# Queries of a latent attention for two batches in one matmul, and its transposed weights in half tiles

## The chip, the cores and the metric

The kernel runs on one core of a Trainium2 chip, as one program. A time is the device time of one execution in microseconds (us). A profile is one execution recorded by the hardware profiler; its span runs from the first to the last instruction.

## What is computed

Two transformer layers on 8 batches of 100 tokens with 512 features: cross attention, a mixture of experts, a second cross attention and a quantised feed-forward layer. The change lies in the second attention ("attention 2"). Cut to it, with b the batch, s the token, l one of 361 context rows, h one of 16 heads, r one of 64 features:

```python
q_r    = einsum('bshq,hqr->bhsr', q_big, W_qr)       # queries, 64 a head
k_r    = einsum('bld,hdr->bhlr', kv_rope, W_kr)      # keys of the turned context
scores = einsum('bhsr,bhlr->bhsl', q_r, k_r)
attn   = softmax(scores)                             # over the 361 rows
ctx_c  = einsum('bhsl,bld->bhsd', attn, kv_rope)
out    = einsum('bhsd,hkd->bshk', ctx_c, w_kc_kv).reshape(b, s, H * K) @ Wo.T
x      = x + out
```

The kernel does not form k_r. It multiplies each head's query by W_kr, which gives a query of 128 features that is scored against the context row itself. That multiplication is what the code calls `queries`.

## The kernel before, in words

Everything is float32 here. `qr` holds the 64 features of all 16 heads for all 800 tokens: even heads in partitions 0 to 63, odd heads in partitions 64 to 127, eight pairs of heads along the second axis. It lies in the upper half of `ctxT`, the tile in which the attention's result is built; a batch's result overwrites the batch's own query columns. `wkr_sb` holds W_kr in the same arrangement.

Attention 2 goes through the batches one after the other (the loop `for b in range(B)`). For a batch:

- `queries(b)` (line 1294): for each of two halves, four pairs of heads; for each pair two matmuls, one with the upper and one with the lower 64 partitions (line 1300; 128 weight columns, 100 moving columns), into two PSUM banks, one for each parity. VectorE copies the even bank (line 1304), ScalarE the odd one (line 1305) into `qe`, 1600 columns: first eight even heads, then eight odd ones. So a batch has 16 matmuls, of which each is two passes of TensorE and two records of the trace, and four copies of 128x400.
- The 1600 columns are cut into 13 tiles, 12 of 128 columns and one of 64 (`BTILES`). `scores` (line 1310): one matmul of the tile's queries against the context columns `kvT`, 361 wide (line 1312); VectorE takes the negative row maximum (line 1314); ScalarE the exponential with its row sum (line 1318); VectorE the reciprocal (line 1320); then VectorE for odd tiles, GpSimd for even ones, multiplies (line 1321).
- `weights_transposed` (line 1324): three transpositions on TensorE (line 1327) and one copy into `pT`, a tile of 3 x 1600 columns, of which there are two.
- `values` (line 1330): when four heads' 400 columns of `pT` are there, three matmuls (line 1333) with the context rows, and a copy into `ctxT`. A batch has four such groups, j = 0 to 3.

The copies of `weights_transposed` and `values` go through `evacuate` (line 77): VectorE (line 80) and ScalarE (line 82) take turns by a counter that runs on over the batches. A batch has 13 + 4 such copies.

The loop runs three tiles ahead: after the scores of tile i, `drain(3)` does the transpositions of tile i - 3, and values that became ready are done with the next transposition. `queries(b + 1)` stands after tile 8 of batch b (after tile 2 in batch 0), and the next context columns are turned after tile 10. In batches 1 and on, after tiles 3 and 9, a late weight block of the feed-forward layer is quantised on VectorE (lines 133 to 145), nine blocks in all.

In this stretch the order written by hand is not enforced: the tile framework's scheduler orders the instructions of each engine when the program is built (the sections before it and the end of the kernel are under `tc.manual_schedule`). Engines run their lists in order and wait for each other on semaphores. [...] After the loop the values are projected (lines 357 and 363) and the feed-forward layer follows.

Of the kernel before, what the change touches and what calls it, by code (L numbers as in the profile page):

```python
# [12 lines left out]
F32 = mybir.dt.float32  # L13
# [6 lines left out]
P = 128  # L20
B, S, D = 8, 100, 512
# [18 lines left out]
NH1, R1, CQ = 16, 64, 384  # L40
LC, LP = 3, 121
# [9 lines left out]
def tile_kernel(  # L51
# [7 lines left out]
    nc = tc.nc  # L59

    def open_pool(name, bufs=1, side="left"):
        guard = tc.tile_pool(name=name, bufs=bufs, side=side)
        pool = guard.__enter__()
        return pool, lambda: guard.__exit__(None, None, None)
# [6 lines left out]
    def bank(dtype=F32):  # L71
        cols = 512 if dtype == F32 else 1024
        return psum.tile([P, cols], dtype, tag="bank", name="bank")
# [3 lines left out]
    def evacuate(dst, src):  # L77
        turn[0] += 1
        if turn[0] % 2:
            nc.vector.tensor_copy(dst, src)  # L80
        else:
            nc.scalar.copy(dst, src)  # L82
# [342 lines left out]
    def columns_of_weights(b):  # L425
        return weights_columns(soft.pop(b)[1])
# [27 lines left out]
    pT = columns_of_weights(0)  # L454
# [3 lines left out]
    for b in range(2, 6):  # L458
# [3 lines left out]
        pT = columns_of_weights(b - 1)  # L462
# [239 lines left out]
    def fold_head(i, wq_p, kq_p, qr_p, j, pa=None):  # L702
        pa = bank() if pa is None else pa
        for c in range(CQ // P):
            nc.tensor.matmul(  # L705
                pa[:, ts(j, R1)], kq_p[:, j, c, :], qr_p[:, j, c, :],
                start=(c == 0), stop=(c == CQ // P - 1),
            )
        return pa

    def fold_copy(i, wq_p, kq_p, qr_p, pa):
        a_p = fw.tile([P, 2 * R1], F32, tag="a_p", name=f"a_p{i}", bufs=2)
        nc.scalar.copy(a_p, pa[:, : 2 * R1])
        return i, wq_p, a_p

    def fold_first(*loads):
        pa = fold_head(*loads, 0)
        return fold_copy(*loads, fold_head(*loads, 1, pa))

    def fold_second(i, wq_p, a_p):  # L720
        pb = bank()
        for j in range(2):
            nc.tensor.matmul(  # L723
                pb[ds(R1 * j, R1), :], a_p[:, ts(j, R1)], wq_p[:, j, :], start=True, stop=True
            )
        f_p = fw.tile([P, D], F32, tag="f_p", name=f"f_p{i}", bufs=2)
        nc.scalar.copy(f_p, pb)
        return i, f_p
# [14 lines left out]
    pT = columns_of_weights(5)  # L743
# [9 lines left out]
    pT = columns_of_weights(6)  # L753
# [12 lines left out]
    pT = columns_of_weights(7)  # L766
# [13 lines left out]
    part = fold_first(*loaded.pop(0))  # L780
# [6 lines left out]
    part = fold_second(*part)  # L787
# [29 lines left out]
    wkr_sb = qw.tile([P, NH1 // 2, DC], F32, tag="wkr", name="wkr_sb")  # L817
# [68 lines left out]
    with tc.If(spills > 0, preferred_fallthrough_block=False):  # L886
# [12 lines left out]
        for e in range(NE):  # L899
# [3 lines left out]
            for t, r in enumerate(ROWS):  # L903
                pt = bank().rearrange("p (c q) -> p c q", c=KC)
# [7 lines left out]
                for m, (m0, mr) in enumerate(HCH):  # L912
                    pw = bank()
                    ups = [(0, UP[m], mr)] if m < 2 else [(0, UP64, 64), (64, HE, 32)]
                    for j, cols in enumerate(([(0, m0, mr)], ups)):
                        a = sp.tile([P, KC, P], F32, tag=f"sp{j}", name=f"sp{j}_{e}_{t}_{m}")
# [5 lines left out]
                        for c in range(KC):  # L922
                            nc.tensor.matmul(
                                pw[:mr, ds(j * P, r)], a[:, c, :mr], xT[:, c, :r],
                                start=(c == 0), stop=(c == KC - 1),
# [111 lines left out]
    part = fold_copy(*loads, fold_head(*loads, 1, pa))  # L1037
    following = fold_first(*loaded.pop(0))
    part = fold_second(*part)
# [6 lines left out]
    for e in range(NE):  # L1046
# [35 lines left out]
        part = None  # L1082
        gate_and_up(0)
        if loaded:
            part = fold_first(*loaded.pop(0))
# [4 lines left out]
        if part:  # L1090
            part = fold_second(*part)
# [90 lines left out]
    qr = ctxT[:, NH1 // 2 :, :]  # L1182
# [21 lines left out]
    for b in range(B):  # L1204
        kv = contexts.pop(0)
        kvr = rot.tile([LP, LC, DC], F32, tag="turned", name=f"turned{b}", bufs=2)
# [11 lines left out]
    def context_rows(b):  # L1218
        kvr = kvp.tile([LP, LC, DC], F32, tag="kvr", name=f"kvr{b}")
        d = nc.sync.dma_start(kvr, ctx_rot[b])  # L1220
        context_load[0] = d.ins
        return kvr

    def context_columns(b, kvr):
        pt = bank()[:, : LC * LP].rearrange("p (c l) -> p c l", c=LC)
        for c in range(LC):
            nc.tensor.transpose(pt[:, c, :], kvr[:, c, :], ident[:LP, :LP])
        kvT = kvp.tile([P, L], F32, tag="kvT", name=f"kvT{b}")
        nc.scalar.copy(kvT[:, :LP], pt[:, 0, :])
        nc.vector.tensor_copy(  # L1230
            kvT[:, LP:].rearrange("p (c l) -> p c l", c=LC - 1), pt[:, 1:, 1:]
        )
        return kvT
# [22 lines left out]
    for g, tiles in enumerate(GROUPS):  # L1256
# [3 lines left out]
        more = g + 1 < len(GROUPS)  # L1260
        if more:
            token_norms(GROUPS[g + 1])
        for p0 in range(0, NH1 // 2, per):
            pq = bank()[:, : per * n].rearrange("p (i q) -> p i q", i=per)
            for i in range(per):
                for c in range(KC):
                    nc.tensor.matmul(  # L1267
                        pq[:, i, :], wqf[:, c, ts(p0 + i, P)], xT[:, c, :],
                        start=(c == 0), stop=(c == KC - 1),
# [9 lines left out]
    kvr = context_rows(0)  # L1279
    kvT = context_columns(0, kvr)  # L1280
# [3 lines left out]
    a1w, close_a1w = open_pool("attn1w", bufs=2)  # L1284
# [4 lines left out]
    HP = NH1 // 2  # L1289
    BROWS = NH1 * S  # L1290
    BTILES = [(k, min(P, BROWS - k)) for k in range(0, BROWS, P)]
    VC = 4 * S

    def queries(b):
        qe = a1w.tile([P, 2, HP * S], F32, tag="qe", name=f"qe{b}")
        for half in range(2):
            pe = [bank(), bank()]
            for i in range(4):
                for par in range(2):
                    nc.tensor.matmul(  # L1300
                        pe[par][:, ts(i, S)], wkr_sb[ds(R1 * par, R1), 4 * half + i, :],
                        qr[ds(R1 * par, R1), 4 * half + i, ts(b, S)], start=True, stop=True,
                    )
            nc.vector.tensor_copy(qe[:, 0, ts(half, VC)], pe[0][:, :VC])
            nc.scalar.copy(qe[:, 1, ts(half, VC)], pe[1][:, :VC])
        return qe.rearrange("p a q -> p (a q)")

    of_scores = []

    def scores(qe, kvT, k0, r, odd):  # L1310
        ps = bank()
        nc.tensor.matmul(ps[:r, :L], qe[:, ds(k0, r)], kvT, start=True, stop=True)  # L1312
        nm = small.tile([P, 1], F32, tag="nm", name="nm")
        d = nc.vector.tensor_reduce(nm[:r], ps[:r, :L], AX.X, ALU.max, negate=True)  # L1314
        of_scores.append(d.ins)
        e = a1w.tile([P, L], F32, tag="e", name="e", bufs=4)
        sm = small.tile([P, 1], F32, tag="sm1", name="sm1")
        nc.scalar.activation(e[:r], ps[:r, :L], AF.Exp, bias=nm[:r], accum_out=sm[:r])  # L1318
        rs = small.tile([P, 1], F32, tag="rs1", name="rs1")
        nc.vector.reciprocal(rs[:r], sm[:r])  # L1320
        (nc.vector if odd else nc.gpsimd).tensor_scalar_mul(e[:r], e[:r], rs[:r])  # L1321
        return e

    def weights_transposed(e, pT, k0, r):
        pt = bank()[:, : LC * P].rearrange("p (c q) -> p c q", c=LC)
        for c in range(LC):
            nc.tensor.transpose(pt[:LP, c, :r], e[:r, ds(c * (LP - 1), LP)], ident[:r, :r])  # L1327
        evacuate(pT[:, :, ds(k0, r)], pt[:LP, :, :r])

    def values(b, j, kvr, pT):  # L1330
        pc = bank()
        for c in range(LC):
            nc.tensor.matmul(  # L1333
                pc[:, :VC], kvr[:, c, :], pT[:, c, ts(j, VC)], start=(c == 0), stop=(c == LC - 1)
            )
        evacuate(
            ctxT.rearrange("p (i a) q -> p i a q", a=2)[:, ts(j % 2, 4), j // 2, ts(b, S)],
            pc[:, :VC].rearrange("p (i q) -> p i q", i=4),
        )
# [5 lines left out]
    def drain(n):  # L1345
        while len(late) > n:
            late.pop(0)()

    def behind(b, i, e, kvr, pT):
        k0, r = BTILES[i]  # L1350
        weights_transposed(e, pT, k0, r)
        while ready:
            values(*ready.pop(0))
        for j in range(NH1 // 4):
            if k0 < (j + 1) * VC <= k0 + r:
                ready.append((b, j, kvr, pT))

    qe = queries(0)
    for b in range(B):
        more = b + 1 < B  # L1360
        pT = a1w.tile([LP, LC, BROWS], F32, tag="pT", name=f"pT{b}")
        if more:
            kvr_next = context_rows(b + 1)
        for i, (k0, r) in enumerate(BTILES):
            e = scores(qe, kvT, k0, r, i % 2)
            late.append(lambda a=(b, i, e, kvr, pT): behind(*a))
            drain(3)
            if more and i == (8 if b else 2):
                qe_next = queries(b + 1)

            if b and i in (3, 9) and late_loads:
                n, w = late_loads.pop(0)
                with tc.issue_after(of_scores[8]):
                    turn_gate_up(*quantise_gate_up(n, w, a1w))
                if n + 2 < OT:
                    with tc.issue_after(context_load[0]):
                        late_loads.append(load_gate_up(n + 2, a1w))
            if more and i == 10:
                kvT_next = context_columns(b + 1, kvr_next)
        if more:  # L1380
            qe, kvr, kvT = qe_next, kvr_next, kvT_next
    drain(0)
    values(*ready.pop(0))
    close_a1w()
# [11 lines left out]
    pt = bank()  # L1396
# [213 lines left out]
    for k, t in enumerate(order):  # L1610
# [8 lines left out]
        if k >= 2:  # L1619
            q, sh = hidden_q.pop(order[k - 2])  # L1620
# [17 lines left out]
    q, sh = hidden_q.pop(last)()  # L1638
# [8 lines left out]
    q, sh = hidden(t, sx, xqT, True)  # L1647
# [81 lines left out]
```

## Time and profile before

| what | value |
|---|---|
| median of 3 runs | 683.59 us (680.39 to 683.71) |
| the profiled execution | 684.2 us |
| its span | 682.5 us |
| granted TensorE clock, mean | 0.981 |
| attention 2, from the first query matmul to the last values | 345.6 to about 539.8 us |
| a batch, from one query block to the next (479.14 to 503.11) | 24.0 us |

How to read the profile. Engines are PE (TensorE matmul), PEld (its weight load), DVE (VectorE), ACT (ScalarE), POOL (GpSimd) and SP (the queue that issues most DMAs). The page gives the busy time of each with its share and the number of instructions, and the chain that ended last: followed back from the last instruction, at each step to what released it. A row of a group of instructions has line, engine, operation, what it writes and reads, shape and count, then busy time in us, mean duration of one in ns, and idle time ahead of it with the releaser. Matmuls are pipelined, so the mean duration of one (272 ns for a query matmul record) is far more than the step from one start to the next; the busy time of the group divided by its count is nearer to what it costs. A wait row reads: who, for whom, total us, how often, longest. A row of the chain reads: start, us, what. A row of the windows reads: window, its length, busy time and count of each engine, granted clock, DMA share, GB/s.

### The profile page before, as it was taken

What the parts mean: (1) busy time and instruction counts of PE and PEld (TensorE: products, weight loads), DVE (VectorE), ACT (ScalarE), POOL (GpSimd) and SP (SyncE); (2) the same over time, 40 slices, a digit from 0 to 9 for tenths busy, and PEclk for the clock granted to TensorE, in tenths of its full rate; (3) what the DMA queues carried; (4) which work ended last, traced back from release to release, by engine and by line L of the source; (5) the groups of instructions that cost most, each with busy time, mean ns of one, the idle gap of its engine ahead of it and who ended that gap; (6) DMA issues with size and microseconds to landing.
All of it is one profiled execution on the core that took longest, in us unless ns stands there. A gap on an engine that the chain in (4) does not pass through costs nothing.

```text
span 682.5 us, 10210 instructions
## 1 busy us (share of the span) xinstructions
PE 647.0 (95%) x3637; PEld 417.3 (61%) x3637; DVE 420.7 (62%) x1059; ACT 245.2 (36%) x557; POOL 184.1 (27%) x197
## 2 busy tenths in 40 slices
PE   8999997499998999999999999999999999999995
PEld 6767755367765677568866666666666644444442
DVE  4875698326665453254168877776676356566687
ACT  3654444141221211231155555455555322221140
POOL 2222231601110022138424243324333102221021
PEclk9999999589999999999999999999999999999998
DMA  8700293699999999664200211110000120111211
GB/s 303 237 17 18 99 331 108 244 301 190 271 288 321 322 254 275 131 193 122 63 1 17 57 44 42 31 35 12 1 11 1 46 83 8 30 29 30 49 37 61
DMA packets 80312, 80.41 MB, mean 118 GB/s; under 512 B 41283, under 2 KB 54135, under 8 KB 80127
## 3 DMA queue, kind: packets, MB, share of 16 engines
q1 hardware_dynamic: 76543, 70.97, 35.8%
q0 software_dynamic: 3712, 8.72, 6.6%
q8 instruction: 30, 0.49, 0.3%
q14 instruction: 27, 0.22, 0.1%
HBM read 56.36 MB, written 16.50 MB: 107 GB/s over the span
## 4 chain that ended last, share of the span: by engine, by line
PE 65%; DVE 7%; DMA 3%; POOL 2%; issue 2%; ACT 1%; SPq 0%; POOLq 0%; ACTq 0%; DVEq 0%
PE bank L357 12%; PE bank L1053 10%; PE bank L1333 10%; PE bank L1312 7%; PE bank L1267 6%; PE bank L1117 5%; PE bank L1327 4%; PE bank L1457 3%; POOL e L1321 2%; PE bank L1300 2%; DVE nm L1314 1%; PE bank L705 1%; PE bank L723 1%; DMA dn<-in_wdn 1%; PE bank L985 1%
## 5 line engine op out<-in xcount | busy, mean ns | idle before, releaser
L1321 POOL TENSOR_SCALAR e<-e,rs 128x361 f32<-128x361 f32 (+1 forms) x56 | 67.3, 1203 | 134.9 <-DVE rs L1320 134.2
L357 PE MATMUL bank<-wvo,ctxT 128*128 128x512 f32 x192 | 83.9, 593 | 0.0
L1312 PE MATMUL bank<-kvT,qe 128*128 128x361 f32 (+1 forms) x208 | 82.0, 477 | 0.0
L1053 PE MATMUL bank<-xgT,w 128*128 128x240 f32 (+1 forms) x384 | 76.5, 371 | 1.6 <-ACT xgT L989 0.9
L1053 PEld LDWEIGHTS bank<-xgT,w 128*128 128x128 f32 (+1 forms) x384 | 63.8, 181 | 16.7 <-issue 9.0
L1333 PE MATMUL bank<-pT,kvr 121*128 121x400 f32 x192 | 70.4, 502 | 1.8 <-DVE pT L80 1.8
L1318 ACT ACTIVATE e<-bank,nm 128x361 f32<-128x361 f32 (+1 forms) x104 | 58.7, 564 | 29.8 <-DVE nm L1314 21.0
L1327 PEld LDWEIGHTS bank<-ident,e 128*121 128x121 f32 (+1 forms) x312 | 47.3, 183 | 33.7 <-POOL e L1321 7.8
L1314 DVE TENSOR_REDUCE nm<-bank 128x1 f32<-128x361 f32 (+1 forms) x104 | 54.9, 528 | 20.3 <-PE bank L1312 19.2
L357 PEld LDWEIGHTS bank<-wvo,ctxT 128*128 128x128 f32 x192 | 36.2, 190 | 43.1 <-issue 42.6
L1128 POOL DMA_INDIRECT x_acc<-y,place x16 | 24.4, 1525 | 128.5 <-ACT y L1127 125.0
L1327 PE MATMUL bank<-ident,e 128*121 128x128 f32 (+1 forms) x312 | 52.8, 279 | 2.1 <-POOL e L1321 2.1
L1474 POOL TENSOR_TENSOR hid<-g,u 128x512 f32<-128x512 f32 (+1 forms) x17 | 20.5, 1214 | 111.1 <-ACT g L1465 74.8
L1333 PEld LDWEIGHTS bank<-pT,kvr 121*128 121x128 f32 x192 | 33.9, 190 | 21.3 <-issue 1.9
L1117 PE MATMUL bank<-w,hT 128*128 128x512 f32 (+3 forms) x96 | 43.3, 596 | 2.2 <-DVE hT L1077 2.2
L1267 PE MATMUL bank<-xT,wqf 128*128 128x256 f32 (+1 forms) x192 | 43.8, 389 | 0.7 <-ACT xT L1252 0.7
L322 POOL TENSOR_TENSOR s<-s,rs 100x800 f32<-100x800 f32 x16 | 24.4, 1523 | 71.2 <-DVE rs L321 30.5
L1267 PEld LDWEIGHTS bank<-xT,wqf 128*128 128x128 f32 x192 | 36.2, 190 | 7.4 <-ACT xT L1252 0.9
L1312 PEld LDWEIGHTS bank<-kvT,qe 128*128 128x128 f32 (+1 forms) x208 | 32.5, 186 | 9.4
L82 ACT COPY pT<-bank 121x384 f32<-121x384 f32 (+1 forms) x51 | 23.7, 465 | 31.9 <-PE bank L1327 31.3
L80 DVE COPY ctxT<-bank 128x400 f32<-128x400 f32 (+2 forms) x23 | 13.2, 574 | 34.1 <-PE bank L1267 24.8
L1117 PEld LDWEIGHTS bank<-w,hT 128*128 128x128 f32 (+3 forms) x96 | 16.8, 183 | 22.9 <-issue 16.4
(251 smaller groups left out, 1020.2 us busy)
## 6 DMA issues: line engine op xcount, KB each, us to landing
w<-in_w SPq DMA_DIRECT2D x8, 1408.0 KB
gu<-in_wgu SPq DMA_DIRECT2D x22, 256.0 KB
w<-in_w SPq DMA_DIRECT2D x16, 256.0 KB
wq_p<-in_wq SPq DMA_DIRECT2D x8, 512.0 KB
wo<-in_wo SPq DMA_DIRECT2D x8, 512.0 KB
x_slot<-zeros SPq DMA_DIRECT2D x1, 3840.0 KB
kq_p<-in_wkcq SPq DMA_DIRECT2D x16, 192.0 KB
dn<-in_wdn SPq DMA_DIRECT2D x4, 704.0 KB
```

Of the source, the lines that this page charges most:

```text
L322: nc.gpsimd.tensor_tensor(part, part, rs.unsqueeze(2).to_broadcast([S, 8, S]), ALU.mult)
L357: nc.tensor.matmul(po[:, :D], lhs[:, c, ds(t * P, r)], rhs[:, c, :], start=(c == 0), stop=(c == chunks - 1),)
L1053: nc.tensor.matmul(po, w12_e[:, c, cols], xgT[:, c, :], start=(c == c0), stop=(c == c1 - 1))
L1117: nc.tensor.matmul(py[i][:n], hT[:mr, m, ds(s0, n)], w3_e[:mr, m, :], start=(m == 0), stop=(m == 2))
L1128: d = nc.gpsimd.indirect_dma_start(out=x_acc, out_offset=bass.IndirectOffsetOnAxis(ap=place[:, 0:1], axis=0), in_=y, in_offset=None, compu ...
L1267: nc.tensor.matmul(pq[:, i, :], wqf[:, c, ts(p0 + i, P)], xT[:, c, :], start=(c == 0), stop=(c == KC - 1),)
L1312: nc.tensor.matmul(ps[:r, :L], qe[:, ds(k0, r)], kvT, start=True, stop=True)
L1314: d = nc.vector.tensor_reduce(nm[:r], ps[:r, :L], AX.X, ALU.max, negate=True)
L1318: nc.scalar.activation(e[:r], ps[:r, :L], AF.Exp, bias=nm[:r], accum_out=sm[:r])
L1321: (nc.vector if odd else nc.gpsimd).tensor_scalar_mul(e[:r], e[:r], rs[:r])
L1327: nc.tensor.transpose(pt[:LP, c, :r], e[:r, ds(c * (LP - 1), LP)], ident[:r, :r])
L1333: nc.tensor.matmul(pc[:, :VC], kvr[:, c, :], pT[:, c, ts(j, VC)], start=(c == 0), stop=(c == LC - 1))
```

## The change

The queries of two batches are made at once. A tile `qe` now holds a pair of batches (2 x 2 x 800 columns, two such tiles). Each matmul takes the 200 moving columns of two neighbouring batches, so a pair of batches has 16 matmuls of 200 columns in place of 32 of 100. They are cut into four parts of two pairs of heads (four matmuls, two copies of 400 columns each with a strided target). The first pair is made ahead of the loop, all four parts at once. The later pairs are made in the odd batch before them: parts 0 and 1 after tile 6, parts 2 and 3 after tile 9. Batch 0 and the other even ones have none.

`pT` is now two tiles of half the columns (800), with three buffers that both halves share, so tile 6, whose columns 768 to 895 lie in both halves, is copied in two pieces, of 32 and 96 columns. A batch has 14 + 4 copies through `evacuate`.

```diff
-    def queries(b):
-        qe = a1w.tile([P, 2, HP * S], F32, tag="qe", name=f"qe{b}")
-        for half in range(2):
+    def pair_tile(b):
+        return a1w.tile([P, 2, 2, HP * S], F32, tag="qe", name=f"qe{b}")
+
+    def queries(b, qe, parts):
+        for part in parts:
             pe = [bank(), bank()]
-            for i in range(4):
+            for i in range(2):
                 for par in range(2):
                     nc.tensor.matmul(
-                        pe[par][:, ts(i, S)], wkr_sb[ds(R1 * par, R1), 4 * half + i, :],
-                        qr[ds(R1 * par, R1), 4 * half + i, ts(b, S)], start=True, stop=True,
+                        pe[par][:, ts(i, 2 * S)], wkr_sb[ds(R1 * par, R1), 2 * part + i, :],
+                        qr[ds(R1 * par, R1), 2 * part + i, ds(b * S, 2 * S)],
+                        start=True, stop=True,
                     )
-            nc.vector.tensor_copy(qe[:, 0, ts(half, VC)], pe[0][:, :VC])
-            nc.scalar.copy(qe[:, 1, ts(half, VC)], pe[1][:, :VC])
-        return qe.rearrange("p a q -> p (a q)")
+            for par, copy in ((0, nc.vector.tensor_copy), (1, nc.scalar.copy)):
+                copy(
+                    qe[:, :, par, ds(2 * part * S, 2 * S)].rearrange("p b (i q) -> p i b q", i=2),
+                    pe[par][:, : 4 * S].rearrange("p (i b q) -> p i b q", i=2, b=2),
+                )
+
+    def of_batch(qe, k):
+        return qe[:, k].rearrange("p a q -> p (a q)")
...
-        evacuate(pT[:, :, ds(k0, r)], pt[:LP, :, :r])
+        for half in range(2):
+            c0, c1 = max(k0, half * 2 * VC), min(k0 + r, (half + 1) * 2 * VC)
+            if c0 < c1:
+                evacuate(
+                    pT[half][:, :, ds(c0 - half * 2 * VC, c1 - c0)], pt[:LP, :, c0 - k0 : c1 - k0]
+                )
 
     def values(b, j, kvr, pT):
+        pT = pT[j // 2][:, :, ts(j % 2, VC)]
...
-                pc[:, :VC], kvr[:, c, :], pT[:, c, ts(j, VC)], start=(c == 0), stop=(c == LC - 1)
+                pc[:, :VC], kvr[:, c, :], pT[:, c, :], start=(c == 0), stop=(c == LC - 1)
...
-    qe = queries(0)
+    pair = pair_tile(0)
+    queries(0, pair, range(HP // 2))
+    qe = of_batch(pair, 0)
...
-        pT = a1w.tile([LP, LC, BROWS], F32, tag="pT", name=f"pT{b}")
+        pT = [
+            a1w.tile([LP, LC, 2 * VC], F32, tag="pT", name=f"pT{b}_{half}", bufs=3)
+            for half in range(2)
+        ]
...
-            if more and i == (8 if b else 2):
-                qe_next = queries(b + 1)
+            if more and b % 2 and i in (6, 9):
+                if i == 6:
+                    pair_next = pair_tile(b + 1)
+                queries(b + 1, pair_next, range(2) if i == 6 else range(2, HP // 2))
...
-            qe, kvr, kvT = qe_next, kvr_next, kvT_next
+            if b % 2:
+                pair = pair_next
+            qe, kvr, kvT = of_batch(pair, (b + 1) % 2), kvr_next, kvT_next
```

## The prediction

> **What bounds the kernel now.** I read the page first: the busy shares, and the chain that ended last.
>
> ```profile
> PE 647.0 (95%) x3637; PEld 417.3 (61%) x3637; DVE 420.7 (62%) x1059; ACT 245.2 (36%) x557; POOL 184.1 (27%) x197
> ...
> PE 65%; DVE 7%; DMA 3%; POOL 2%; issue 2%; ACT 1%; SPq 0%; POOLq 0%; ACTq 0%; DVEq 0%
> ```
>
> TensorE bounds the whole. The change touches only attention 2, so the second view is the busy time in that stretch, 345 to 545 us, of all engines and then of the query matmuls (L1300) alone (window, its length, then busy time and count of PE, PEld, DVE, ACT, POOL):
>
> ```profile
> 345.00:545.00 200.00, 196.05 (x1127) 130.13 (x1126) 142.48 (x398) 107.16 (x304) 67.27 (x56) 1.00 0.09 24
> ```
> ```profile
> 345.00:545.00 200.00, 16.26 (x256) 14.91 (x256) 1.00 0.09 24
> ```
>
> TensorE is idle 3.95 us of 200 at full clock: what it is spared here ends the stage earlier. The queries hold 16.26 us, 8 batches of 2.03. The next view is what TensorE waits for in this stretch:
>
> ```profile
> PE bank L1327 <- POOL e L1321: 2.1, 9, 0.6
> PE bank L1333 <- DVE pT L80: 1.8, 4, 0.5
> ```
>
> The first is mostly 0.2 us where a batch begins; the second is 0.44 us in batches 1 and 3 each, and 0.42 and 0.54 at the very end. The chain shows one query block of the steady part, and then the wait of batch 1:
>
> ```profile
> 406.63 0.33 PE bank L1327 x3
> 406.96 1.96 PE bank L1300 x32
> 408.92 0.80 PE bank L1312 x2
> 409.73 0.33 PE bank L1327 x3
> 410.05 0.61 PE bank L1312 x2
> ```
> ```profile
> 384.10 1.25 DVE gu_q L141 x2
> 385.35 0.48 DVE qe L1304
> 385.83 0.44 DVE nm L1314
> 386.27 0.48 DVE pT L80
> 386.75 0.14 issue
> 386.88 2.25 PE bank L1333 x6
> ```
>
> The 32 records of a block are 16 matmuls of two passes, all on the chain, and the scores behind them take 0.80 instead of 0.61. In batch 1 the second group of values (j = 1) waits for a transposed tile that VectorE copies only after a weight quantisation and a query copy.
>
> **The change part by part: wider query matmuls.** Taken singly, the record starts of a block come in pairs 7 ns apart (the two halves of the array's rows, L1300 alternates between them), and a pair follows a pair after 112 ns. One pass of 100 columns streams in less: the values take 2.02 us for 6 passes of 400 columns, 0.842 ns a column, so 84 ns. What sets 112? These rows have 128 weight columns like L1300:
>
> ```profile
> L269 PE MATMUL bank<-xnT,wq_sb 128*128 128x200 f32 x96 | 17.3, 337 | 0.5 <-ACT xnT L254 0.5
> L1300 PE MATMUL bank<-ctxT,wkr_sb 64*128 64x100 f32 x256 | 16.3, 277 | 0.0
> L705 PE MATMUL bank<-qr_p,kq_p 128*128 128x64 f32 x96 | 14.4, 310 | 8.1 <-issue 8.1
> L296 PE MATMUL bank<-kT,qT 32*100 32x100 f32 x256 | 7.7, 257 | 0.0
> L269 PE MATMUL bank<-xnT,wq_sb 128*128 128x100 f32 x64 | 7.3, 275 | 0.0
> ```
>
> The commonest step from start to start is 112 ns at 64 columns (L705), 112 at 100 (L269) and 169 at 200 (L269). [...] L296 shows that row groups stream side by side: four of them start within 20 ns and the next four 68 ns after that, 88 in all, the time of one pass. I take 169 ns for a pair at 200 columns.
>
> [...] L705 and L269 are this case's own, with the same count of weight columns, so I take them.
>
> A block also has edges: the last transposition before it reaches its successor after 202 ns instead of 109, the first pair after 190 instead of 112, the last pair after 209, and the first score pass behind it takes 407 instead of 305. Together 370 ns. [...] So:
> - before, a block is 16 x 112 + 370 = 2.16 us, two batches 4.32;
> - after, the odd batch has two blocks of 8 pairs, 8 x 169 + 370 = 1.72 each, 3.44 together.
> That spares 0.88 us in each of three pairs (batches 2 and 3, 4 and 5, 6 and 7): **2.6 us**.
>
> **The first pair.** Before, two blocks at the start, 4.3 us; after, one, 16 x 169 + 370 = 3.07. But here the other engines end last: the first transposition started at 353.00, after the first product on POOL, 351.55 to 352.75. After the change VectorE makes four query copies (0.56) ahead of the first row maximum instead of two, and ACT four ahead of its table load (1.28). By the row times the last query copy on ACT ends near 349.2, the table is there at 350.5, the first exponential and its sum at 351.15, the reciprocal behind four maxima at 351.5, and POOL starts about 351.6, as before. The chain decides here: between nothing and the 1.25 us of TensorE work I take **0.2 us** of gain, since the second pair of copies in the way of the first tiles is gone.
>
> **The copies.** Two batches had four VectorE copies of 128x400 (0.564 us, L1304) and four on ACT (0.492). They have as many now, with a strided target. The ctxT copies, of the same size and strided, took 0.575 and 0.492: no change. They move from one place in each batch to two in the odd one. Nothing is queued on POOL or SP: the built kernel has the same order on both, and the step issues no DMA.
>
> **Half tiles.** Tile 6 (columns 768 to 896) straddles the halves, so one copy of 384 columns (0.544 on VectorE, 0.477 on ACT) becomes two, of 3 x 32 = 96 and 3 x 96 = 288. The 64-row tile's 192 took 0.338 and 0.318, so 0.16 us more per 192 columns, and the 96 near 0.25 and the 288 near 0.44: 0.2 us more work, 8 times, beside TensorE. If that cover were gone it would cost 1.6 us. Two consequences: every batch from 1 on now has an even number of copies, so the turns no longer flip, and in the built order the 96-column piece falls to ACT, the 288 to VectorE. The values of j = 1 need only the first half, so only the ACT piece. That is the wait of batches 1 and 3 (0.44 each): its VectorE copy is out of the way, and a query block of 1.72 us now stands between the transposition and these values. I count **0.9 us** of gain. With three half buffers the tile written is always one whose values ended half a batch ago: no wait on TensorE.
>
> **New waits.** In the built order VectorE's 288-column copy waits for ACT's piece, behind it reciprocals and the next maxima. ACT reaches it after an exponential (0.56 + 0.20), so up to 1 us of VectorE idleness in each batch. And in batches 1 and 3 two query copies fall into the quantisation. From the maximum of tile 6 to that of tile 9 VectorE's list holds 4 maxima (2.12), 3 reciprocals (0.48), 2 quantised weights (3.9: maximum 0.67, scale 0.14, inverse 0.15, product 0.41, rounding 0.58, each twice, from the timeline), 2 query copies (1.12), 2 products (0.92) and 2 transposed copies (1.08): 9.6 us in single durations, near 7.8 since starts overlap by some 0.08. TensorE has 6.6 us in the same stretch (a block 1.72, one group of values 2.02, 3 scores 1.83, 3 transpositions 0.99). VectorE falls 1.2 to 3.0 us back. The transposition of tile 8 comes two tiles, a block and more values later, 12.5 us after the score of tile 6; its weights are ready after maximum (8.6), exponential, reciprocal and POOL product (2.1), so 10.7: margin 1.8 us. Between 0 and 2.6 us (0.44, the wait seen before, at each of six blocks) I take **0.4**, one such wait, as the margin is positive but rests on summed durations.
>
> **Sum.** -2.6 - 0.2 - 0.9 + 0.4 = -3.3 us. TensorE is 93% busy after the stage as well, and the chain goes through it there (values projection, L357), so the gain is kept. The profiled execution took 684.2 (span 682.5): 680.9. The median of the runs is 0.6 below it, 683.59: **680.3**.
>
> **The rivals.**
> - *The pace is as said, but waits eat it.* VectorE stays late in odd batches and the 0.44 us wait appears at each of six blocks, with the old two kept: -2.6 - 0.2 + 2.6 = -0.2, 683.4; three of the six give 682.1. For it: VectorE is already in the chain of batch 1. Against it: the margin of 1.8 us. I expect its form of three, 682.1.
> [...]
> - *Slower: two row groups don't stream side by side beyond 100 columns.* Then a pair is 2 x 169 = 338 ns in place of 169, at each of 64 pairs (16 for each pair of batches): 64 x 169 = 10.8 us more, of which at most 1 us hides at the start; -3.3 + 9.8 = +6.5, 690. It decides from a pair step of 169 + 3300 / 64 = 221 ns on. For it: no row shows 64-row halves with 200 columns. Against it: 112 is already less than the 168 that two passes of 100 in series need, and L296.
> - *VectorE becomes the bound of odd batches.* If it falls 1.8 us further back than summed, TensorE waits for each microsecond above it; 2 us in three batches is +6 - 3.3: 686.3. For it: the new wait on ACT. Against it: only 71% busy in the stage.
>
> **How the numbers follow.** The sum 0.52, with its own range 678.5 to 682 (0.4 may be 0, the first pair may give 1.25; or the 0.9 may not come); waits eat it 0.30; no floor 0.06; serial halves 0.05; VectorE bound 0.07. The runs before spread over 3.3 us, so the median itself can sit 2 us off. Range: 677.5 to 684.8. A measurement of this kernel tells from no change about 0.5%, 3.4 us. The sum lies at that border: faster by more 0.41 (two in three of the sum's cases, a fifth of the second's), within it 0.49, slower 0.10.
>
> **What would show it.** L1303 (as L1300 is then called): 256 records become 128, a step of 169 ns within them and some 11.5 us busy in place of 16.3; the two chain pieces of an odd batch near 1.5 us each. A step over 221 makes it wrong at once. TensorE's wait for VectorE's transposed copies falls from 1.8 to about 1.0 us (the end stays). The first transposition keeps its distance to the first query, 7.4 us. If the step is right and the time is not, the waits of TensorE between the blocks of batches 1, 3 and 5 hold the rest, and the row to look at is VectorE's copy behind ACT.

## The result

| | before | after |
|---|---|---|
| median of 22 runs each | 682.42 us (680.39 to 683.71) | 678.34 us (677.0 to 685.36) |
| ratio | | 0.9942, 95% interval 0.9931 to 0.9954 |
| profiled execution, span | 684.2, 682.5 us | 679.23, 677.5 us |
| start of the trace to the first query matmul | 345.58 us | 344.79 us |
| **stretch**: first query matmul to first matmul of the values' projection | 194.29 us | 190.15 us |
| from there to the last matmul | 135.24 us | 135.21 us |

The changed kernel is 4.1 us faster, 0.58%; the forecast was 3.3. The profiled executions differ by 5.0 us in span, of which 0.79 lies ahead of everything that was changed. That part lay between 344.8 and 350.9 us in the profiles of this study; it is not the change's. The stretch is: -4.15 us. The end did not move. All comparisons of traces below are of the stretch.

The page of after, busy shares and chain by engine:

```profile
PE 644.1 (95%) x3502; PEld 415.6 (61%) x3509; DVE 419.1 (62%) x1063; ACT 245.4 (36%) x561; POOL 184.2 (27%) x197
...
PE 68%; DVE 5%; DMA 2%; issue 2%; POOL 1%; ACT 1%; SPq 1%; ACTq 0%; POOLq 0%; DVEq 0%
```

TensorE remains the bound. The same window as before, 345 to 545 us, for the query matmuls alone (now L1303), and their row by shape:

```profile
345.00:545.00 200.00, 12.51 (x128) 10.35 (x126) 1.00 0.11 32
```
```profile
L1303 PE MATMUL bank<-ctxT,wkr_sb 64*128 64x200 f32 x128 | 12.7, 340 | 0.0
```

Half the records (256 before) and 12.7 us in place of 16.3 (the window cuts 0.2 us off the first block). From start to start a pair of records takes 169 to 170 ns (7 and then 162 or 163).

What TensorE waits for in that window:

```profile
PE bank L1336 <- POOL e L1330: 3.5, 6, 2.3
PE bank L1348 <- DVE pT L80: 1.1, 3, 0.5
```

The second row fell from 1.8, to near the 1.0 that was forecast. The first rose from 2.1, but its composition changed: 2.3 and 0.46 us now fall at the very start, and the waits of 0.2 us, of which before had one in each of batches 1 to 7, are left only in batches 2, 4, 6 and 7. These two pieces of after's chain show why. First batch 6, which has no query block; then batch 5, which has two:

```profile
494.28 0.62 PE bank L1321 x2
...
494.93 0.53 DVE nm L1323
...
495.72 1.20 POOL e L1330
...
496.96 0.59 PE bank L1336 x3
497.55 0.67 PE bank L1348 x2
```
```profile
471.07 0.33 PE bank L1336 x3
471.39 1.55 PE bank L1303 x16
472.95 0.81 PE bank L1321 x2
473.75 0.33 PE bank L1336 x3
```

A batch's values come after every third tile, except once, where four tiles lie between two groups of values. There the transposition of tile 4, which stands behind the score of tile 7, follows its own score so soon that maximum, exponential, reciprocal and GpSimd's product (1.20) end last: this is "the wait at tile 4" below. A query block after tile 6 stands just ahead of it, and the wait is gone.

Such a wait costs more than the idle time that the profile gives. Taken singly, the score ahead of it is followed after 304 + 343 to 361 ns, and the first transposition behind it takes 99 ns more than its neighbours: 0.44 us for "0.2". The values' wait of batch 1, "0.44", costs 0.60 + 0.08 = 0.68. The modelled end of a matmul covers the difference.

### The profile page after: what moved, and what is told of

Same layout as the page of the kernel before. It is cut to its first block, busy times and chain, and to the rows that moved or that the text cites. A ratio compares the mean times of both kernels' runs of the same rounds, so it can differ in the third digit from the quotient of the medians.

```text
span 677.5 us, 9955 instructions
## 1 busy us (share of the span) xinstructions
PE 644.1 (95%) x3502; PEld 415.6 (61%) x3509; DVE 419.1 (62%) x1063; ACT 245.4 (36%) x561; POOL 184.2 (27%) x197
## 4 chain that ended last, share of the span: by engine, by line
PE 68%; DVE 5%; DMA 2%; issue 2%; POOL 1%; ACT 1%; SPq 1%; ACTq 0%; POOLq 0%; DVEq 0%
PE bank L357 12%; PE bank L1053 11%; PE bank L1348 9%; PE bank L1321 8%; PE bank L1267 6%; PE bank L1117 6%; PE bank L1336 5%; PE bank L1481 3%; PE bank L1303 2%; PE bank L705 1%; PE bank L723 1%; PE bank L985 1%; POOL e L1330 1%; DMA sin_sb<-in_rope_sin 1%; DVE nm L1323 1%
## 5 line engine op out<-in xcount | busy, mean ns | idle before, releaser
L82 ACT COPY pT<-bank 121x384 f32<-121x384 f32 (+1 forms) x63 | 28.3, 449 | 42.0 <-PE bank L1336 41.9
L80 DVE COPY ctxT<-bank 128x400 f32<-128x400 f32 (+2 forms) x31 | 17.7, 572 | 36.8 <-PE bank L1267 25.8
L1065 DVE TENSOR_TENSOR hT<-silu,bank 128x240 f32<-128x240 f32 x16 | 6.5, 404 | 39.5 <-ACT silu L1064 39.5
```

## The experiments

Each was timed beside the kernel before on its own chip (whose median of before was 686.2 to 687.1 in these), so ratios are compared. The stretch is from its one profiled execution. Where an interval holds 1, or overlaps that of the kernel it is set against, the reading rests on the traces alone; from the first values on, two traces of the changed kernel differ by 0.08 us.

| kernel | ratio to before, 95% interval | stretch, us | against before | queries after the first values | waits after them |
|---|---|---|---|---|---|
| before | 1 | 194.29 | | 12.98 | 5.08 |
| after | 0.9942 (0.9931 to 0.9954) | 190.15 | -4.15 | 10.54 | 3.04 |
| after, again | 0.9944 (0.9924 to 0.9964) | 191.02 | -3.27 | 10.54 | 2.95 |
| half tiles alone | 0.9999 (0.998 to 1.0017) | 192.97 | -1.32 | 12.98 | 3.81 |
| old queries at tile 6 | 0.9992 (0.9978 to 1.0006) | 193.38 | -0.91 | 12.99 | 4.59 |
| half tiles, queries at tile 6 | 0.9981 (0.9961 to 1.0001) | 192.40 | -1.89 | 12.98 | 3.31 |
| after, 100 columns | 0.9992 (0.9982 to 1.0002) | 193.48 | -0.81 | 12.98 | 3.09 |
| after, one place, tile 8 | 0.992 (0.9898 to 0.9942) | 190.25 | -4.04 | 9.33 | 4.05 |
| after, one place, tile 6 | 0.9929 (0.9907 to 0.995) | 190.62 | -3.67 | 9.33 | 4.50 |
| after, first pair in two | 0.992 (0.9897 to 0.9942) | 189.15 | -5.14 | 10.54 | 2.98 |
| the same, context at tile 6 in even batches | 0.9892 (0.987 to 0.9913) | 188.39 | -5.90 | 10.54 | 2.64 |
| first pair in two, context at tile 6, queries at tile 8 | 0.9905 (0.9877 to 0.9934) | 188.51 | -5.78 | 9.33 | 3.85 |
| before, context at tile 6 | 0.9985 (0.9962 to 1.0008) | 193.14 | -1.15 | 12.99 | 4.69 |

(The last two columns are summed from the record starts: steps into, within and out of query blocks, and what steps between other matmuls take beyond their common length where that is over 0.13 us.)

**Half tiles alone.** In the kernel before, only `pT` and its copies change:

```diff
-        pT = a1w.tile([LP, LC, BROWS], F32, tag="pT", name=f"pT{b}")
+        pT = [
+            a1w.tile([LP, LC, 2 * VC], F32, tag="pT", name=f"pT{b}_{half}", bufs=3)
+            for half in range(2)
+        ]
```

> The kernel before with the transposed weights in half tiles, nothing else. Counted against before. Theory (the half tile takes VectorE's late copy out of the way of the values j = 1 in batches 1 and 3; a wait there costs 0.68 us from start to start): about -1.3 us; the waits of the transposition of tile 4 for GpSimd (0.44 us from start to start in each of batches 1 to 7) all stay. Rival a (those waits went because the copies' turns no longer flip): another -1.3 us, three of them gone. Rival b (the values' wait went because the queries were moved): 0, both waits stay.

```profile
PE bank L1327 <- POOL e L1321: 2.2, 9, 0.6
PE bank L1339 <- DVE pT L80: 1.0, 2, 0.5
```

The stretch is 1.32 us shorter; both values' waits are gone from the trace (the two that are left lie at the very end), and all seven waits at tile 4 are there. So the theory holds in the trace and rivals a and b fall. The times alone do not tell 1.3 us from nothing: the interval reaches from -1.4 to +1.2 us.

**Old queries at tile 6.**

```diff
-            if more and i == (8 if b else 2):
+            if more and i == (6 if b else 2):
```

> The kernel before with its one query block of each batch after tile 6 instead of tile 8, nothing else. Theory (whatever TensorE does between the transpositions of tiles 3 and 4 gives GpSimd's product its time): the wait at tile 4 goes in batches 1 to 6, 6 x 0.44 = -2.6 us, and stays in batch 7; the values' waits in batches 1 and 3 stay, as the full tile still ends with VectorE's copy. Rival a: no change at tile 4, 0 us. Rival b (the values' waits go by the place): -4.0 us.

Six of seven waits at tile 4 are gone, batch 7's is left: the theory's mechanism. But it gained 0.91 us and not 2.6, since the values' waits grew (0.86 and 0.75 in batches 1 and 3, from 0.60 each) and new ones came in batch 2 (0.87) and, small, in 4 and 5. What they wait for is VectorE's copy of tile 6's transposition. Moving the block away from tile 8 took it out from between the score of tile 8 and these values. In batch 1, VectorE had done the maximum of tile 8 before the block (382.12 us in the trace of before), and of the maxima only tile 9's stood between the quantised weights and this copy. With the block after tile 6, the maxima of tiles 8 and 9 and a reciprocal that waits for ScalarE (387.20) stand there, and the copy starts at 387.28. For times, 0.91 us is too little to be told from nothing.

**Half tiles, queries at tile 6.** Both edits.

> The kernel before with half tiles and with its query block after tile 6; queries still one batch at a time, 100 columns. Theory: both effects add, -2.6 - 1.3 = -3.9 us, so almost all of the measured gain (-4.1) without one wider matmul. Rival (the wider matmuls are most of the gain): -1.5 us or less.

1.89 us and not 3.9, nearer the rival's 1.5: the effects don't add. The values' waits are there again in batches 1 to 3 (0.74, 0.43, 0.49), by this row of its waits:

```profile
PE bank L1339 <- DVE nm L1314: 1.2, 3, 0.6
```

The half tile's small piece is copied by ScalarE, which takes it after an exponential, which waits for VectorE's maximum, which stands behind the weight quantisation. The half tile removed one way to VectorE and left another. In batch 1 that copy started at 389.01 us and the values at 389.29. In the changed kernel it is the second query block, after tile 9, that covers this: TensorE is in it from 384.59 to 386.15, and the small copy (385.93, 0.23 us) is done before the values' turn at 387.19.

**After, 100 columns.**

```diff
-                for par in range(2):
-                    nc.tensor.matmul(
-                        pe[par][:, ts(i, 2 * S)], wkr_sb[ds(R1 * par, R1), 2 * part + i, :],
-                        qr[ds(R1 * par, R1), 2 * part + i, ds(b * S, 2 * S)],
-                        start=True, stop=True,
-                    )
+                for k in range(2):
+                    for par in range(2):
+                        nc.tensor.matmul(
+                            pe[par][:, ts(2 * i + k, S)], wkr_sb[ds(R1 * par, R1), 2 * part + i, :],
+                            qr[ds(R1 * par, R1), 2 * part + i, ts(b + k, S)],
+                            start=True, stop=True,
+                        )
```

> The changed kernel with each 200-column query matmul made as two of 100 columns, in the same places and with the same copies. Theory (a pair of matmuls costs its 112 ns weight load at 100 columns, 169 at 200): 16 x (224 - 169) = 0.88 us for each of three pairs of batches, and part of it in the first: +2.6 to +3.5 us against the changed kernel, so -1.5 to -0.6 against before. [...]

It gives back 3.33 us of the stretch (193.48 against 190.15): 2.44 in the query blocks, 0.85 at the start. Its query row:

```profile
L1304 PE MATMUL bank<-ctxT,wkr_sb 64*128 64x100 f32 x256 | 16.0, 276 | 0.0
```

So the width is worth four fifths of the gain, and the times say the same (0.9992 against 0.9942, intervals apart). A cost in proportion to the columns is ruled out: 100 columns cost 112 ns here, not half of 169. By the rows, with 128 weight columns the step is 112 ns at 8 moving columns (L600), at 64 (L705) and at 100 alike, and L296 with 100 weight and 100 moving columns takes 88. That the load of the weights sets the 112 was the author's estimate; no run changed the weight columns alone.

**One place, tile 8, and one place, tile 6.**

```diff
-            if more and b % 2 and i in (6, 9):
-                if i == 6:
-                    pair_next = pair_tile(b + 1)
-                queries(b + 1, pair_next, range(2) if i == 6 else range(2, HP // 2))
+            if more and b % 2 and i == 8:
+                pair_next = pair_tile(b + 1)
+                queries(b + 1, pair_next, range(HP // 2))
```

(6 in place of 8 in the second.)

> The changed kernel with all four query parts of a pair after tile 8 of the odd batch, the old place. Counted against the changed kernel. Theory: the waits at tile 4 come back in batches 1, 3 and 5 (3 x 0.44 = +1.3), one block's edges of 0.39 less in each (-1.2): +0.1 us, so -4.0 against before; the waits are seen in the trace. Rival (two places are needed because VectorE and the banks can't take eight copies at once): new waits of TensorE behind the block, +2 us or more.

> The changed kernel with all four query parts of a pair after tile 6 of the odd batch. Theory: no wait at tile 4, and one block's edges less in each of three batches: -1.2 us against the changed kernel, -5.3 against before. Rival (VectorE and the banks can't take eight copies at once beside the quantisation): a wait behind the block in batches 1 and 3, +1 us or more against the changed kernel.

At tile 8: +0.10 us of stretch against after, as expected, out of 1.21 less in the blocks (one block's edges, 0.40, three times), and the waits at tile 4 back in batches 1, 3 and 5. Two places are not needed for VectorE's sake. At tile 6: +0.47, neither the theory's -1.2 nor the rival's +1, but by the rival's kind of wait. The waits at tile 4 stay away in batches 1, 3 and 5, but the values of batches 1 and 3 wait 0.74 and 0.81:

```profile
PE bank L1348 <- DVE nm L1323: 1.2, 2, 0.6
```

All four query copies of VectorE and two quantised blocks stand ahead of the maxima there, and no block follows before those values. The changed kernel's two places each cover a wait, and pay a second pair of edges for it.

**The first pair in two.**

```diff
-    queries(0, pair, range(HP // 2))
+    queries(0, pair, range(2))
...
+            if b == 0 and i == 2:
+                queries(0, pair, range(2, HP // 2))
```

> The changed kernel with the first pair's queries cut in two: parts 0 and 1 ahead of the loop, parts 2 and 3 after the scores of tile 2. Theory (the start lost 0.7 us against before, as four copies and four maxima now stand on VectorE ahead of the first reciprocal): the first transposition comes 1 us or more sooner after the first query; one block's edges more (0.39): -0.6 us against the changed kernel. Rival (the start waits on the table load and GpSimd whatever the order): 0 or +0.4 us.

From the first query to the first values it takes 11.84 us in place of 12.77 (before: 12.06); the stretch is 1.0 us shorter, more than the 0.6 expected. The first transposition comes 7.21 us after the first query, 0.67 sooner than in the changed kernel. What was lost at the start is seen in after's chain:

```profile
344.86 2.91 PE bank L1303 x32
347.76 2.64 PE bank L1321 x8
...
351.21 1.41 POOL e L1330
...
353.29 0.56 DVE pT L80
353.85 0.14 DVE rs L1329 x2
...
354.01 1.20 POOL e L1330
...
355.26 0.59 PE bank L1336 x3
```

Four maxima stand ahead of the first reciprocal, and then VectorE's list has the first transposed copy ahead of the reciprocals of tiles 2 and 3. GpSimd's second product, tile 2's, can't start before the first transposition has been copied (353.29 to 353.85), though its exponential was done at 351.4.

**The context turned after tile 6**, in even batches of the kernel with the first pair in two, in all batches of before, and in all batches with the queries after tile 8.

```diff
-            if more and i == 10:
+            if more and i == (10 if b % 2 else 6):
                 kvT_next = context_columns(b + 1, kvr_next)
```

> As the kernel with the first pair cut in two, and in even batches the next context columns are turned after tile 6 instead of tile 10: 0.3 us of TensorE work between the transpositions of tiles 3 and 4, where these batches have no query block. Theory (any work there gives GpSimd's product its time): the waits at tile 4 of batches 2, 4 and 6 shrink or go, up to 3 x 0.44 = -1.3 us against the kernel with the first pair cut in two. Rival (the wait ends with GpSimd, which the turn doesn't move, and the copies of the turn delay the maxima): 0 or slower.

> The kernel before with the next context columns turned after tile 6 instead of tile 10 in every batch, nothing else: 0.3 us of TensorE work between the transpositions of tiles 3 and 4. Theory (any work there gives GpSimd's product its time): the waits at tile 4 go or fall by 0.3 us in batches 1 to 6, up to 6 x 0.44 = -2.6 us; where the rows of the next context land late, a wait for their DMA takes their place (about 0.3 us was seen in two batches), so between -1.3 and -2.6. Batch 0 has its wait too and may gain 0.4. Rival (the wait at tile 4 went in the changed kernel because a block of queries is long, 1.7 us): 0.3 us of work does nothing, 0.

> The first pair cut in two, the next context columns turned after tile 6 in every batch, and all four query parts of a pair after tile 8 of the odd batch: one block's edges (0.39) less in each of three batches, and no wait at tile 4 for them to cure. Theory: -1.2 us against the kernel with two query places and the turn at tile 6 in even batches, so -7 us against before, stretch near 187.2. Rival (eight copies at once beside the quantisation): new waits behind the block in batches 1 and 3, the gain is lost.

In even batches it brings 0.76 us more, and the ratio 0.9892 is clear of the changed kernel's. The wait at tile 4 goes wherever the turn is put (batch 7, which has none, keeps it). In batch 6 the turn's three tenths of a microsecond of TensorE work are enough alone: the wait there falls from 0.36 to 0.03 us. In batches 2 and 4 the turn comes too soon and waits itself, 0.29 and 0.47 us longer than a step without a wait, so the full 1.3 is not reached. Before with the turn at tile 6 gains 1.15, under the expected 1.3 to 2.6 and, in times, not to be told from nothing; all six of its turns wait, 0.15 to 0.53 us. In the kernel with the queries at tile 8 as well:

```profile
PE bank L1227 <- DMA kvr<-ctx_rot: 1.0, 3, 0.5
```

The next context's rows have two buffers and can only be loaded once the last batch's final values are read. With the queries at tile 8 as well, the blocks are 1.21 us shorter and the waits 1.21 longer: stretch 188.51 against 188.39, no gain, the expected 187.2 missed. The best kernel of the study is the one with the context turned at tile 6 in even batches, 1.1% faster than before (0.9 to 1.3): some 7.4 us, of which its trace shows 5.9 in the stretch.

**After, again.**

> The changed kernel again, on the chip of the two that follow. The stretch from the first query matmul to the first matmul of the values' projection was 190.15 us, 4.15 less than before; if the stretch is a property of the program it comes out within 0.3 us again. The time stands at 0.994 of before.

The time repeats; the stretch is 0.87 us longer, outside the 0.3 expected. The whole difference lies before the first values (13.73 against 12.77 us); from there on it is 177.3 in both. The cause, the clock, is in the last section.

## Why the prediction was right, and where not

The time lies in the range (680.3 forecast, 678.34 measured; the fuller runs put before itself at 682.42, so the change is -4.1 for -3.3). The measured time is just under 678.5, the lower end that the sum had for itself. That the total came so near is in part luck: the start lost 0.9 us against its forecast, and 1.3 were gained that nobody had counted. The forecast lay just inside the 0.5% taken as the border, the measurement just past it. By its steps:

- **Wider matmuls, -2.6: right.** 169 ns a pair as taken from L269; a block of eight pairs with its edges 1.75 us (1.72 said; the edges are 395 ns for 370). Steady blocks: 10.54 for 12.98, -2.44. The strided copies take 564 and 493 ns, as before.
- **The first pair, -0.2: wrong, +0.71.** The step that failed is "the second pair of copies in the way of the first tiles is gone". Those copies were gone, but VectorE's list had four maxima ahead of the first reciprocal (first transposition 7.88 us after the first query, not 7.4: +0.45) and a transposed copy ahead of the third (TensorE's second wait 0.46 us, not 0.20: +0.26). The list of the changed kernel showed both; only the first was counted, and GpSimd's first product still began 6.42 us after the first query where 6.0 was reckoned. The end of that product before the change was also misread: 352.95, not 352.75. Cutting the pair gave 0.93 back.
- **The half tiles, -0.9: right in kind, under-sized.** The waits of batches 1 and 3 went, worth 1.35: the profile's idle time was taken as their cost. Half tiles alone give 1.32. That a query block has to stand ahead of these values was part of the forecast, and the runs bear it out: with the one block moved to tile 6 the half tile takes off 0.98 us (193.38 to 192.40), but waits of 0.43 to 0.74 us stay in batches 1 to 3.
- **New waits, +0.4: the size was right by luck, the place not.** None at the query blocks. One of 0.41 in batch 2: its third group of values waits for tile 9's copy on VectorE, behind the quantised weights.
- **Not foreseen, -1.3.** The waits at tile 4 in batches 1, 3 and 5. They were in the prediction's own wait row (2.1 us, nine times), put down to the start of a batch and left standing. Asking which two matmuls each lay between would have shown that the query block had been moved into the gap.

The sum of the trace: +0.71 - 2.44 - 1.35 - 1.33 + 0.41 = -4.0 of -4.15; the rest is under 0.1 us each. Of the rivals, waits did not eat the gain; a cost in proportion to the columns ("no floor" among the chances) fell with the 100-column kernel (112 ns at 100 columns, 169 at 200); row groups do stream side by side at 200 columns (169 ns, not 338); VectorE did not bound the odd batches in this form; with one place at tile 6 its waits come.

Not tried: the pair tile with full-width `pT` (two of those take 9.6 KB a partition more than the three half tiles), so what half tiles are worth within the changed kernel stays open.

## What to carry to other kernels

A float32 pass of 8, 64 or 100 moving columns cost the same 112 ns in this kernel, one of 200 cost 169. Find the step from start to start at two widths in a kernel's own rows, and widen where the step does not grow with the width. Where the bound engine has short waits at fixed places of a loop, ask which other work of its own can be moved into each; a block that must be done anyway hides a latency for nothing, and moving it uncovers the place that it came from. Price a wait by the steps between starts, not by the idle time in the row.

## What was not expected of the hardware

In the start's pause TensorE waits 2.27 us (0.61 before). In the second profiled execution of the changed kernel the granted clock (third column from the end) falls to a half shortly after this pause; stretches of 2 us:

```profile
354.00:356.00 2.00, 0.01 (x1) 0.01 (x1) 0.83 (x4) 1.25 (x6) 1.40 (x1) 1.00 0.00 0
356.00:358.00 2.00, 2.00 (x9) 1.70 (x10) 1.35 (x5) 0.02 (x1) 0.66 (x1) 0.74 0.00 0
358.00:360.00 2.00, 2.00 (x6) 1.33 (x6) 0.97 (x4) 1.20 (x4) 0.58 (x2) 0.50 0.01 4
```

The half clock lasted from 356.95 to 360.37, 3.41 us, in which a score pass took 600 ns instead of 305 and a transposition 213 instead of 109; the first values came 0.96 us later than in the first execution. In the 3.41 us ahead of the drop TensorE had stood still for 2.3, two thirds.

The same pause of 2.27 us lies in the first execution from 350.39 to 352.66, and the granted clock is 1.00 in each stretch of 2 us from 350 to 358. So the pause alone does not tell whether the clock falls. In the traces of before and after the clock also falls to a half near 120 us: from 121.05 to 141.53 in before, from 120.00 to 143.89 in after. What sets off a drop was not shown, and no run was made for it. In the kernel with the first pair in two the longest of these waits at the start is 0.7 us, and the granted clock is 1.00 from 352 to 358 us.
